# Two graph-attention layers on one core: bias vectors loaded as rows, late broadcasts, and a new order of the first and last pairs

## The chip, the cores and the metric

The kernel runs on one core of one Trainium2 chip. The metric is device time in microseconds (us), the median over runs; lower is better. The engines are TensorE (PE, with its weight loads shown apart as PEld), VectorE (DVE), ScalarE (ACT), GpSimd (POOL) and SyncE (SP, which here only issues DMA transfers). ACT and POOL can issue transfers too, each on a queue of its own.

## The reference

The input x holds 128 graphs of 128 nodes with 512 features, all in float32. Two layers follow each other.

```
q, k, v = x @ Wq + bq, x @ Wk + bk, x @ Wv + bv        # 8 heads of 64
attn    = softmax(q k^T / 8 + (adj - 1) * 1e9)
y       = layernorm(x + (attn v) @ Wo + bo)
h       = y @ W
e       = leaky_relu(h a1 (rows) + h a2 (columns)) * adj
out     = layernorm(y + elu(softmax(e) h + beta * h))
```

`adj` is one 128 x 128 matrix of zeros and ones for all graphs, `a` is split into a1 and a2, `beta` is one number.

## The kernel before

The graphs are worked on in pairs: 64 pairs (`NG`), g = 0 to 63, each of graphs b0 and b1. The five products with 512 x 512 weights (named q, k, v, w for Wo, h for W) are done in seven block products each instead of eight, after a scheme of sums and differences of blocks. `product(name, g, n)` issues the block product n (1 to 7) on PE; `block_sum` makes the sums of the activations on POOL; `weight_sum(name, n, engine)` makes the sums of the weights, once, at the start: those of q and k on DVE, those of v, w and h on POOL. `take_part` moves a block of the result out of PSUM (on ACT for q, k, v and h, with the bias for q and k; on DVE for w), and `add_block` adds a second block to it on DVE.

A pair passes through these steps: its blocks of x are loaded (`fetch_blocks`, into a single buffer `xblk`) and turned by DVE (`turn_x`); the products of q and k; `scores` on PE; `mask` and `row_max` on DVE; `exps` and `normalise` on ACT; a write to DRAM and a read back that moves blocks (`attn_write`, `attn_read`), turned by DVE (`turn_attn`); v's products; `attend` on PE and `attend_evict` on ACT with v's bias; w's products; `residual`, which adds bo to x on POOL; the first layer norm; the edge weights of the second layer (`row_product`, `edge`, `leaky`, `weights`); `aggregate`; h's products; the ELU and the second layer norm; the store. In the last pair some products are done plainly (`plain`, `end_product`), since a second copy of half a weight can be loaded over a weight that is done with (`load_again`).

The order of the work is written out by hand as a list of pieces, each with a place, which is a number. `at(place, fn, ...)` records a piece, and at the end all pieces are sorted by place and issued in that order. A place is only a key: nothing on the chip waits for it, but each engine works through its own pieces in that order. The pair g has its places at `g * STEP + place` with STEP = 36.678. `rows(g)` holds the places of an ordinary pair; `other` holds tables of places of its own for pairs 0, 1, 2, 3, 60 and 61, in the order of `rows(g)`; `last_rows(g)` holds the pieces and places of pairs 62 and 63. The weights and constants of the start are recorded one by one below them (lines 1098 to 1137).

The loads of the start, by queue:

- SP: half of the first pair's blocks (L81), Wq (L99), then, behind a `memset` on DVE that follows the first `turn_x` (`load_k_and_v`, L205), Wk and Wv; then x of the first pair, the second pair's blocks, W and Wo (L119).
- ACT: the other half of the first pair's blocks.
- POOL: two columns for the biases of q and k (`column`, L107: 512 numbers spread over 128 partitions, four on each), `adj`, and then `load_later` (L150), placed at the very start: the column for v's bias and the broadcasts of beta, a1, a2 and bo to all partitions (`broadcast`, L102).

The first user of the biases is `take_part` (L352) for q and k and `attend_evict` (L463) for v. `make_beta` (L167) uses beta, `wa_column` (L175, eight pieces on DVE), `wa_turn` (PE) and `wa_centre` (DVE) turn W and a into two rows; bo is used by `residual` (L429). `keep_busy` (L131) issues 15 matmuls of the identity with itself on PE at the start, whose result nobody reads.

Of the kernel before, what the change touches and what calls it, by code (L numbers as in the profile page):

```python
# [8 lines left out]
F32 = mybir.dt.float32  # L9
# [4 lines left out]
P = 128  # L14
# [8 lines left out]
def gnn_two_layers(  # L23
# [34 lines left out]
    nc = tc.nc  # L58
# [48 lines left out]
    def column(src, name):  # L107
        t = cpool.tile([P, NC], F32, tag=name, name=name)
        nc.gpsimd.dma_start(out=t, in_=src.rearrange("(c p) -> p c", p=P))
        return t  # L110

    wv_sb, wq_sb, wk_sb = turned("wv_sb"), turned("wq_sb"), turned("wk_sb")
    xblk, xn = {0: load_blocks(0)}, {}
    load_turned(wq_sb, wq)
# [16 lines left out]
    def keep_busy(n, name):  # L131

        t = ps_mm.tile([P, P], F32, tag="mm", name=name)
        for _ in range(n):
            nc.tensor.matmul(t, ident, ident, start=True, stop=True)

    keep_busy(15, "early")
    mhalf = cpool.tile([P, G], F32, tag="mhalf", name="mhalf")
    nc.gpsimd.memset(mhalf, -0.5)
    bq_c = column(bq, "bq_c")  # L140
    bk_c = column(bk, "bk_c")
# [8 lines left out]
    def load_later():  # L150
        later["bv"] = column(bv, "bv_c")
# [306 lines left out]
    def attend_evict(b):  # L458

        oT[b] = wk2.tile([P, NC, N], F32, tag="oT", name=f"oT_{b}")  # L460
        src = po.pop(b)
        for c in range(NC):
            nc.scalar.activation(  # L463
                oT[b][:, c, :], src[:, c, :], AF.Identity, bias=later["bv"][:, c : c + 1]
            )
# [352 lines left out]
    def last_rows(g):  # L818

        b0, b1 = g * G, g * G + 1  # L820
        if g == NG - 2:
# [4 lines left out]
                (-24.602, product, "q", g, 1), (-21.007, take_part, "q", g, 1, 0, 0),  # L826
                (-20.065, product, "q", g, 6), (-18.272, product, "q", g, 7),
                (-17.379, product, "k", g, 7), (-17.337, take_part, "q", g, 6, 1, 0),
                (-16.541, fetch_x, b0), (-16.486, product, "q", g, 2), (-16.091, fetch_x, b1),
                (-15.593, product, "k", g, 1), (-14.7, product, "k", g, 2),  # L830
                (-12.947, take_part, "k", g, 1, 0, 0), (-12.481, add_block, "q", g, 2, 0, 0),
                (-12.121, add_block, "k", g, 2, 0, 0), (-10.901, residual, b0),
                (-9.651, residual, b1), (-9.477, product, "q", g, 5),
                (-8.344, take_part, "q", g, 5, 1, 1), (-7.718, product, "k", g, 6),
                (-6.585, take_part, "k", g, 6, 1, 0), (-5.093, product, "k", g, 5),
                (-3.799, take_part, "k", g, 5, 1, 1), (-3.334, product, "q", g, 3),
                (-2.499, add_block, "k", g, 7, 1, 1), (-2.441, product, "k", g, 3),
                (-2.201, take_part, "q", g, 3, 0, 1), (-2.139, add_block, "q", g, 7, 1, 1),
                (-1.548, product, "k", g, 4), (-1.308, take_part, "k", g, 3, 0, 1),
                (-0.655, product, "q", g, 4), (0.478, add_block, "q", g, 4, 1, 0),  # L840
                (1.178, add_block, "k", g, 4, 1, 0), (2.175, scores, b1), (3.322, scores, b0),
                (3.562, mask, b1, 0), (4.182, mask, b1, 1), (4.222, product, "v", g, 1),
                (4.802, mask, b0, 0), (5.285, product, "v", g, 2), (5.422, mask, b0, 1),
                (6.042, row_max, b0), (6.391, take_part, "v", g, 1, 0, 0), (7.182, row_max, b1),
                (7.382, exps, b0, 0), (7.883, product, "v", g, 6), (8.152, exps, b0, 1),
                (8.922, exps, b0, 2), (9.122, add_block, "v", g, 2, 0, 0), (9.692, exps, b0, 3),
                (10.462, exps, b1, 0), (10.481, product, "v", g, 7), (10.682, row_inv, b0),
                (11.232, exps, b1, 1), (12.002, exps, b1, 2), (12.772, exps, b1, 3),
                (13.793, row_inv, b1), (15.553, normalise, b0, 0), (16.143, normalise, b0, 1),
# [322 lines left out]
```

## Time and profile before

| what | value |
|---|---|
| median of 3 runs | 2377.96 us (2376.72 to 2378.68) |
| the profiled execution | 2381.36 us |
| its span, from first to last instruction | 2379.6 us |
| PE busy | 2353.9 us (99%) |
| DVE busy | 1960.5 us (82%) |
| ACT busy | 1589.5 us (67%) |
| POOL busy | 867.7 us (36%) |
| moved by DMA | 269.83 MB, mean 113 GB/s |

The page of the profile gives the busy time of each engine, the chain of work that ended last, followed back from the last instruction, and the costliest groups of instructions. Beside it the trace answers questions: the timeline lists instructions in order of time with their start, their duration and, in brackets, how long the engine had been idle before and what released it; busy time can be asked for any stretch of the span; the view of the DMA queues gives packets, megabytes and the share of the 16 DMA engines' time, also for a stretch. The queues are q1 for SP, q10 for ACT and q0 for POOL. "x30" after a line is a count of instructions; a float32 matmul appears as two.

### The profile page before, as it was taken

Reading aid. Unit: us, or ns where it says so; the run is one execution under the profiler, and the core shown is the slowest. Engines: PE = TensorE matmul, PEld = TensorE weight load, DVE = VectorE, ACT = ScalarE, POOL = GpSimd, SP = SyncE. Lnnn points to the kernel's source line nnn. Section 1 sums busy time; section 2 is a strip of 40 time slices with the busy share of each in tenths; the row PEclk is TensorE's granted clock in tenths of the full one; section 3 lists DMA queues with packets and bytes.
Section 4 is the critical chain, followed back from the end, with each engine's and each line's share of the span. In section 5 each row is a group of like instructions: output and inputs, shape, how many; then the busy total and the mean of one; then the engine's idle time right before and its main releaser. Section 6 shows DMA issues by size and latency. Waiting matters only on the chain.

```text
span 2379.6 us, 50867 instructions
## 1 busy us (share of the span) xinstructions
PE 2353.9 (99%) x17702; PEld 2177.3 (91%) x17702; DVE 1960.5 (82%) x4390; ACT 1589.5 (67%) x5762; POOL 867.7 (36%) x1047
## 2 busy tenths in 40 slices
PE   8999999999999999999999999999999999999997
PEld 7999899999999999999999999999999999999986
DVE  6787788888888888888888888888888888888887
ACT  4675666766766667667666676676666766766765
POOL 6243333433433334334333333343343333433432
PEclk9999999999999999999999999999999999999999
DMA  6333334334333343343433433424434334333432
GB/s 192 107 92 119 111 107 125 95 118 128 97 119 116 105 122 103 109 134 92 120 119 103 122 108 109 127 91 121 123 102 118 110 109 125 96 117 124 114 115 73
DMA packets 256193, 269.83 MB, mean 113 GB/s; under 512 B 57456, under 2 KB 204912, under 8 KB 255552
## 3 DMA queue, kind: packets, MB, share of 16 engines
q1 hardware_dynamic: 254992, 265.45, 37.1%
q8 instruction: 140, 2.29, 0.4%
q0 software_dynamic: 400, 0.86, 0.1%
q14 instruction: 117, 0.96, 0.1%
q10 hardware_dynamic: 544, 0.26, 0.0%
HBM read 157.62 MB, written 108.85 MB: 112 GB/s over the span
## 4 chain that ended last, share of the span: by engine, by line
PE 95%; DMA 2%; DVE 1%; ACT 1%; issue 0%; SPq 0%; POOLq 0%; POOL 0%; ACTq 0%; DVEq 0%
PE pk L304 12%; PE pq L304 12%; PE pv L298 12%; PE ph L298 11%; PE pw L298 11%; PE eq L304 9%; PE psc L376 5%; PE po L451 5%; PE pz L639 5%; PE eh L298 4%; PE ew L298 4%; PE ev L298 4%; DMA w_sb<-in_L_gnn_W_dram 1%; DMA wk_sb<-in_L_gnn_Wk_dram 0%; DMA scr<-sb 0%
## 5 line engine op out<-in xcount | busy, mean ns | idle before, releaser
L432 POOL TENSOR_TENSOR x<-x,bo_b_in 128x512 f32<-128x512 f32 x128 | 163.3, 1277 | 858.6 <-DMA x<-in_x_dram 858.6
L398 ACT ACTIVATE s<-s,nmax 128x128 f32<-128x128 f32 x1024 | 396.9, 396 | 58.3 <-DVE nmax L392 58.2
L412 ACT ACTIVATE sb<-s,rinv 128x128 f32<-128x128 f32 x1024 | 325.2, 392 | 0.4 <-DVE rinv L405 0.4
L352 ACT ACTIVATE kT<-pk,bk_c 128x128 f32<-128x128 f32 x512 | 159.7, 363 | 204.3 <-PE pk L304 146.2
L352 ACT ACTIVATE qT<-pq,bq_c 128x128 f32<-128x128 f32 x512 | 160.1, 367 | 156.7 <-PE pq L304 156.7
L502 DVE SCALAR_TENSOR_TENSOR ya<-w,wa_row 128x512 f32<-128x512 f32 x256 | 223.9, 874 | 4.4
L398 ACT ACTIVATION_READ_ACCUMULATOR s<-s,nmax 128x1 f32 x1024 | 199.2, 195 | 0.0
L463 ACT ACTIVATE oT<-po,bv_c 128x128 f32<-128x128 f32 x512 | 139.1, 382 | 80.2 <-PE po L451 80.1
L349 DVE TENSOR_TENSOR w<-pw,x 128x256 f32<-128x256 f32 x252 | 106.4, 422 | 99.8 <-PE pw L298 94.0
L441 DVE STREAM_TRANSPOSE attnT<-ab 128x512 f32<-128x512 f32 x256 | 172.6, 693 | 7.5 <-DMA ab<-scr 7.2
L384 DVE SCALAR_TENSOR_TENSOR s<-psc,amask 128x512 f32<-128x512 f32 x256 | 168.7, 681 | 0.8 <-PE psc L376 0.8
L392 DVE TENSOR_REDUCE nmax<-s 128x8 f32<-128x1024 f32 x128 | 156.1, 1220 | 4.4
L346 ACT COPY h<-ph 128x256 f32<-128x256 f32 x252 | 93.7, 372 | 94.9 <-PE ph L298 94.7
L346 ACT COPY v<-pv 128x256 f32<-128x256 f32 x256 | 94.4, 369 | 86.4 <-PE pv L298 59.9
L237 DVE STREAM_TRANSPOSE xT<-xblk 128x512 f32<-128x512 f32 x128 | 139.7, 1110 | 6.2 <-DMA xblk<-in_x_dram 6.2
L257 POOL TENSOR_TENSOR tx<-xT 128x256 f32<-128x256 f32 x128 | 95.6, 748 | 124.3 <-PE psc L376 104.3
L654 DVE SCALAR_TENSOR_TENSOR u<-h,x 128x512 f32<-128x512 f32 x126 | 87.1, 691 | 63.7 <-ACT h L346 61.6
L304 PE MATMUL pq<-xT,wq_sb 128*128 128x128 f32 x1024 | 135.1, 275 | 3.0 <-DMA wq_sb<-in_L_gnn_Wq_dram 3.0
L304 PE MATMUL pk<-xT,wk_sb 128*128 128x128 f32 x1024 | 135.9, 277 | 2.1 <-DMA wk_sb<-in_L_gnn_Wk_dram 2.1
L298 PE MATMUL pv<-wv_sb,xT 128*128 128x256 f32 x512 | 137.5, 392 | 0.0
L304 PEld LDWEIGHTS pk<-xT,wk_sb 128*128 128x128 f32 x1024 | 130.2, 193 | 5.5 <-DMA wk_sb<-in_L_gnn_Wk_dram 2.3
L304 PEld LDWEIGHTS pq<-xT,wq_sb 128*128 128x128 f32 x1024 | 129.3, 192 | 6.4 <-issue 3.2
(677 smaller groups left out, 6349.8 us busy)
## 6 DMA issues: line engine op xcount, KB each, us to landing
scr<-sb SPq DMA_DIRECT2D x128, 512.0 KB
ab<-scr SPq DMA_DIRECT2D x512, 128.0 KB
x<-in_x_dram SPq DMA_DIRECT2D x128, 256.0 KB
xblk<-in_x_dram SPq DMA_DIRECT2D x254, 128.0 KB
out_dram<-u SPq DMA_DIRECT2D x126, 256.0 KB
pb<-s2d SPq DMA_DIRECT2D x62, 128.0 KB
attd<-att SPq DMA_DIRECT2D x62, 128.0 KB
ab<-attd SPq DMA_DIRECT2D x248, 32.0 KB
```

What stands on the lines that cost most here:

```text
L237: nc.vector.transpose(xT[g][:, :, t * N : (t + 1) * N].rearrange("p m (b r) -> p b m r", r=Q), xblk[g][:, t].rearrange("p b (c m) -> p b m ...
L298: nc.tensor.matmul(out, b[:, c, :], a[:, c, :], start=first and c == 0, stop=(c == 1), skip_group_check=True,)
L304: nc.tensor.matmul(out[:, m * N : (m + 1) * N], a[:, c, m * P : (m + 1) * P], b[:, c, :], start=first and m == 0 and c == 0, stop=(c == 1) ...
L346: nc.scalar.copy(dst, src)
L352: nc.scalar.activation(dst[:, m, :], src[:, m * N : (m + 1) * N], AF.Identity, bias=BIAS[name][:, 2 * i + m : 2 * i + m + 1],)
L384: nc.vector.scalar_tensor_tensor(s_t[b][:, j * HP : (j + 1) * HP, :], psc[b][j], SCALE, amask.rearrange("p (o n) -> p o n", o=1).broadcast ...
L392: nc.vector.tensor_reduce(nmax[b], s_t[b], AX.X, ALU.max, negate=True)
L398: nc.scalar.activation(s_t[b][:, h, :], s_t[b][:, h, :], AF.Exp, bias=nmax[b][:, h : h + 1], accum_out=rsum[b][:, h : h + 1],)
L412: nc.scalar.mul(sb[b][:, :, h, :], s_t[b][:, h, :].rearrange("p (b c) -> p b c", c=Q), rinv[b][:, h : h + 1],)
L432: nc.gpsimd.tensor_tensor(xr[b], xr[b], later["bo"], ALU.add)
L441: nc.vector.transpose(attnT[b].rearrange("p h (a r) -> p a h r", r=Q)[:, rows], ab[b].rearrange("p a (h c) -> p a h c", c=Q)[:, rows],)
L502: nc.vector.scalar_tensor_tensor(z, y[b], 1.0, wa_row[j], ALU.mult, ALU.mult, accum_out=s12[g][:, i, j : j + 1])
```

## The change

The three biases of q, k and v are no longer loaded as columns by POOL. They are loaded as 12 rows of 128 numbers by ACT's queue, behind its half of the first blocks; PE turns them behind the matmuls of `keep_busy`, in the same PSUM tile, and ACT copies the 128 x 12 result to SBUF. Slices of it serve as the three bias columns.

`load_later` now holds only the four broadcasts, and moves from the first place to a place behind the last of v's weight sums. With it move the pieces that use what it loads: `make_beta`, all eight `wa_column`, both `wa_turn` and `wa_centre`, and the `residual` pieces of the first two pairs. Wo is loaded before W, and the second pair's blocks are fetched before the second x.

The places of the first pairs (0 and 1 wholly, 2 and 3 in part) and of the last four (60 and 61 from some place on, 62 and 63 wholly) are other numbers. The pieces themselves are the same ones, apart from those named above. Pairs 4 to 59 keep their places.

```diff
-    def column(src, name):
-        t = cpool.tile([P, NC], F32, tag=name, name=name)
-        nc.gpsimd.dma_start(out=t, in_=src.rearrange("(c p) -> p c", p=P))
-        return t
-
     wv_sb, wq_sb, wk_sb = turned("wv_sb"), turned("wq_sb"), turned("wk_sb")
     xblk, xn = {0: load_blocks(0)}, {}
+
+    bias_rows = cpool.tile([3 * NC, P], F32, tag="bias_rows", name="bias_rows")
+    for i, src in enumerate((bq, bk, bv)):
+        nc.scalar.dma_start(
+            out=bias_rows[i * NC : (i + 1) * NC], in_=src.rearrange("(c p) -> c p", p=P)
+        )
     load_turned(wq_sb, wq)
...
-
-    keep_busy(15, "early")
+        return t
+
+    early = keep_busy(15, "early")
+    nc.tensor.transpose(early[:, : 3 * NC], bias_rows, ident[: 3 * NC, : 3 * NC])
+    bias_c = cpool.tile([P, 3 * NC], F32, tag="bias_c", name="bias_c")
+    nc.scalar.copy(bias_c, early[:, : 3 * NC])
     mhalf = cpool.tile([P, G], F32, tag="mhalf", name="mhalf")
     nc.gpsimd.memset(mhalf, -0.5)
-    bq_c = column(bq, "bq_c")
-    bk_c = column(bk, "bk_c")
+    bq_c, bk_c, bv_c = (bias_c[:, i * NC : (i + 1) * NC] for i in range(3))
...
     def load_later():
-        later["bv"] = column(bv, "bv_c")
         later["beta"] = broadcast(cpool, beta, 1, "beta_b")
...
-                oT[b][:, c, :], src[:, c, :], AF.Identity, bias=later["bv"][:, c : c + 1]
+                oT[b][:, c, :], src[:, c, :], AF.Identity, bias=bv_c[:, c : c + 1]
...
-            (20.046, turn_attn, b0, 0), (20.106, normalise, b1, 3), (20.666, turn_attn, b0, 1),
+            (20.404, normalise, b1, 2), (20.484, turn_attn, b0, 0), (20.994, normalise, b1, 3),
...
-            (62.027, end_store, b1, 1), (62.477, end_store, b1, 0),
+            (62.815, end_store, b1, 1), (63.265, end_store, b1, 0),
...
-    at(0.583, load_later)
-    at(5.685, load_k_and_v)
-    at(8.723, weight_sum, "q", 3, nc.vector)
...
-    at(12.183, make_beta)
-    at(13.163, weight_sum, "k", 3, nc.vector)
...
-    at(16.043, make_mask)
-    at(16.793, load_weight, w1_sb, w1)
-    at(19.323, weight_sum, "v", 3, nc.gpsimd)
-    at(19.493, load_weight, wo_sb, wo)
...
-    at(21.883, wa_column, 0, 0)
-    at(22.613, wa_column, 0, 1)
...
-    at(24.623, wa_column, 0, 3)
-    at(25.353, weight_sum, "v", 4, nc.gpsimd)
...
-    at(38.807, wa_centre, 1)
...
+    at(3.885, load_k_and_v)
+    at(6.923, weight_sum, "q", 3, nc.vector)
...
+    at(10.383, make_mask)
+    at(11.363, weight_sum, "k", 3, nc.vector)
...
+    at(14.243, weight_sum, "v", 3, nc.gpsimd)
+    at(14.293, load_weight, wo_sb, wo)
...
+    at(17.693, load_weight, w1_sb, w1)
+    at(18.863, weight_sum, "v", 4, nc.gpsimd)
+    at(20.143, load_later)
...
+    at(31.963, make_beta)
+    at(32.483, wa_column, 0, 2)
...
+    at(38.463, wa_centre, 0)
+    at(43.373, wa_column, 1, 0)
+    at(44.303, weight_sum, "h", 1, nc.gpsimd)
+    at(44.303, wa_turn, 1)
+    at(45.493, wa_centre, 1)
```

## The prediction

> **What bounds the kernel now.** I read the page first: PE is busy 99% of the span and carries 95% of the chain that ended last, so only stretches in which PE idles, or works on nothing useful, can give time back. Busy time by stretch shows where they are: from 200 to 2200 us PE is busy 1997.06 of 2000 us, and the losses sit in the first 60 us and in the last 60. The rows below are such stretches (us from the start, then PE, PEld, DVE, ACT and POOL busy, PE clock, DMA share, GB/s).
>
> ```profile
> 0.00:11.20 11.20, 5.51 (x31) 5.35 (x31) 2.25 (x4) 1.28 (x1) 8.80 (x21) 1.00 0.69 183
> 11.20:20.70 9.50, 7.40 (x48) 7.20 (x49) 6.17 (x11) 1.25 (x4) 0.00 (x0) 0.82 1.03 343
> ...
> 28.80:54.00 25.20, 23.89 (x188) 21.85 (x186) 23.74 (x45) 16.64 (x68) 17.20 (x16) 1.00 0.47 128
> 54.00:70.00 16.00, 16.00 (x134) 14.31 (x133) 12.16 (x24) 12.88 (x56) 5.57 (x8) 1.00 0.31 98
> 15.00:20.00 5.00, 3.70 (x20) 3.71 (x21) 2.90 (x5) 0.43 (x2) 0.00 (x0) 0.69 1.05 314
> ```
>
> Before 11.2 us PE does only warming matmuls. From 11.2 to 20.7 it lacks 2.1 us, and from 15 to 20 its clock was 0.69. From 28.8 to 54 DVE is busy 23.74 of 25.2 us: there DVE is nearly as tight as PE, which is the main doubt below. From 54 us PE is full.
>
> The timeline of the start names what PE waited for:
>
> ```profile
> 1.31 0.93 POOL L109 DMA_DIRECT2D bq_c<-in_L_gnn_bq_dram  x1 [0.34 <-issue]
> ...
> 2.69 5.51 PE L135 MATMUL early<-ident 128*128 128x128 f32 x30 [2.69 <-POOL ident masks.py:199]
> ...
> 11.20 1.13 PE L304 MATMUL pq<-xT,wq_sb 128*128 128x128 f32 x8 [3.00 <-DMA wq_sb<-in_L_gnn_Wq_dram]
> ...
> 16.30 3.23 PE L304 MATMUL pk<-xT,wk_sb 128*128 128x128 f32 x16 [2.10 <-DMA wk_sb<-in_L_gnn_Wk_dram]
> ...
> 19.32 1.55 PE L304 MATMUL pq<-tx,s_q 128*128 128x128 f32 x8
> ...
> 20.70 1.06 PE L304 MATMUL eq<-tx,s_k 128*128 128x128 f32 x8
> ```
>
> The first useful product runs at 11.20, when Wq has landed; the fourth, at 16.30, when Wk has. After these two waits the clock is low: the three products k1, k2, q6 (k1 being product 1 of k) take 16.30 to 20.70 = 4.40 us, where three take 3 x 0.893 = 2.68 later. Why Wq needs from 1.67 (issue) to 11.08 is in the DMA view by queue, from 6 to 8 us and from 8 to 10 us (packets, MB, share of the 16 engines):
>
> ```profile
> q1 hardware_dynamic: 49, 0.34, 44.6%
> q0 software_dynamic: 57, 0.02, 39.1%
> ```
>
> ```profile
> q0 software_dynamic: 91, 0.11, 35.4%
> q1 hardware_dynamic: 26, 0.16, 20.9%
> ```
>
> POOL's queue (q0) takes 39.1% and 35.4% of the engines while it moves 0.02 and 0.11 MB: what it carries first are the three bias columns, 2 KB each, that landed 7.7 to 8.2 us after issue. Wq meanwhile falls from 0.48 MB in 4 to 6 us to 0.34 and 0.16 MB.
>
> At the other end of the run the timeline shows DVE's turn of the attention waiting for its round trip through DRAM, and PE behind it:
>
> ```profile
> 2326.22 0.34 SPq L419 DMA_DIRECT2D scr<-sb  x1
> ...
> 2335.82 1.30 DVE L441 STREAM_TRANSPOSE attnT<-ab 128x512 f32<-128x512 f32 x2 [2.29 <-DMA ab<-scr]
> ...
> 2337.22 0.43 PE L533 MATMUL pb<-ident,s_in 128*128 128x128 f32 x2 [1.60 <-DVE s_in L510]
> ```
>
> **What the skill says.** "DMA: Bandwidth & Descriptors", Specifications, gives 512 B as the smallest transfer for line rate, with a read-modify-write below; the columns are pieces of 4 B, and the trace agrees (39.1% of the engines for 0.02 MB). The same page, Queues, rings and completion order: each DMA engine takes turns between its queues, packet by packet; so POOL's packets slow SP's, as q1's fall shows. Its section on the anatomy of a GpSimd-issued DMA prices one at 2.0 us + bytes / 436 GB/s, 2.6 us for 256 KB; here such broadcasts took 10.1 to 14.2 us beside SP's backlog, so that is only the lower bound. "TensorE: Matmul & The Clock Gate", Part 1: an idle window of about 3.4 us halves the clock, sustained work restores it; the 0.69 after waits of 3.0 and 2.1 us agrees.
>
> **The change part by part.**
>
> 1. Bias loads. Three column loads leave POOL (0.93 + 0.79 + 0.75 = 2.47 us of issue, no one waits there) and become three row loads on ACT's queue, 12 runs of 512 B. ACT issued two loads in 0.93 us, so three cost 1.4 us of an ACT that is idle until 9.06. Added: one small transpose on PE behind the warming matmuls (the nearest row, four of them for the weight vectors, took 0.68 us: 0.2) and one ACT copy (0.4, with its table load of 1.28 ahead of it). The copy runs at about 8.5 to 10, ahead of the first eviction of q, which is not yet due. Cost on the path: 0.2.
>
> 2. Wq. By 6 us SP's queue has moved half of it: 0.30 MB in 2 to 4 us, less 0.26 of the first blocks, and 0.48 in 4 to 6. The other 0.53 MB takes 1.3 us at 410 GB/s (0.61 MB at 74.9% in 12 to 14 us) or 2.2 at the 243 of 4 to 6 us: landing at 7.5 to 8.8 with about half a microsecond to complete; I take 8.2. PE's warming ends at 8.20 anyway, so the first product starts at 8.5: **-2.7** (-2.4 to -2.9).
>
> 3. Wk. The broadcasts (0.77 MB), issued at the start in the kernel before, are gone from this stretch too. 1.05 MB at 410 GB/s is 2.6 us, at 270 3.9: landing at 10.8 to 12.1 after Wq. PE reaches it after three products, 8.5 + 2.7 = 11.2, so the wait of 2.10 becomes 0 to 0.9: **-2.1 + 0.2**.
>
> 4. Clock. With no idle of that length left the 4.40 - 2.68 = **-1.7** come back (0 if a wait of 2 us stays).
>
> 5. The new order of the first pairs. Up to place 60 both orders hold the same 57 PE pieces, 50.8 us of work; in the trace they take from 11.20 to 68.66, so 6.6 us are lost: 2.1 and 1.7 as above, 0.35 + 0.42 + 0.88 waiting for evictions and sums, 1.2 in small gaps. I keep the last four. New is DVE's load: `make_beta`, eight `wa_column` (0.69 to 1.41 each, 0.77 mostly) and two `wa_centre` (2.0) now come between places 31.9 and 47.5, where three columns were done by 24.6. DVE's work between places 30 and 50, by durations from the timeline: 7 block additions of 0.42, 2 masks of 0.65, 4 half turns of the attention of 0.65, 2 turns of x of 1.1, 8 columns of 0.77, 2 centrings of 2.0, two reciprocals and `make_beta` of 0.7 in all, 19.9 us in 20 us of places; before, with 9 additions, 3 masks and 5 columns, 18.9. Against that, DVE is idle about 11 us between 5 and 28 and gets Wq and Wk earlier, and the columns run beside less POOL work. Cost 0 to 3, I take **+1.3**: what is late is the sum of k4 of the second pair, and with it the scores of the third.
>
> 6. `load_later` behind v's sums. Four broadcast issues (0.55 + 1.08 + 0.54 = 2.2 us) come on POOL after Wv (2.6 us after Wk, about 13.8), four sums of 1.3 and a block sum of 0.75, at 19.8 to 22. Behind them on POOL are Wo's sums, not needed before 50. First to need them is `make_beta`, behind the first reciprocal on DVE (39.32 before, about 33.5 then); with latencies of 8.4 to 11.5 they land at 28 to 33. Cost 0, covered by 0 to 5 us. The residuals that wait for bo move to place 37.6 and later; before, POOL stood 11.06 us at one of them with v's sums behind it.
>
> 7. SP's queue. The second pair's blocks now go ahead of the second x, Wo ahead of W. All land earlier, since 0.77 MB of broadcasts and the columns are behind or gone: Wo from 32.9 to about 20 (Wv at 13.8, then 1.8 MB of x, blocks and Wo at the 290 GB/s of 20.7 to 28.8 us). Cost 0.
>
> 8. Middle: the same rows, PE full; 0.
>
> 9. Last pairs. Same PE work. The keys of the order end 0.8 later (63.265 against 62.477), which bounds the loss by order alone. But the transfers decide the middle of this stretch: the write of the first attention is placed at 12.752 against 12.773, so the turn still comes near 2335.8 less the head's gain; from `spread_s2` on both orders have 36.3 us of PE work and gaps by their places. **+0.1**, from -1.0 to +1.2.
>
> Sum: -2.7 - 2.1 + 0.2 - 1.7 + 0.2 + 1.3 + 0.1 = -4.7. The profiled execution took 2381.36 us (span 2379.6, 1.8 around it), 3.4 above the median shown; it would be 2376.7, and the median 2377.96 - 4.7 = **2373.3**. A run differs from another of this kernel by up to 0.1%, so about 0.2% (4.8 us) is what can be told from no change: the forecast stands on that line.
>
> **Rivals.**
>
> A, full gain: DVE keeps up. For it speaks its early idle. -6.0: 2371.9.
>
> B, DVE becomes the bound between 30 and 50 us: its 23.74 of 25.2 us speak for it. Then the part of the head's gain that exceeds DVE's own earlier start is lost, about 3 to 4 us: 2376.2.
>
> C, the columns were not what held Wq: the first blocks' 512 B runs and the 243 GB/s speak for it, q0's 39.1% against. Half of 2, 3 and 4 is left, -3.2 + 1.6 = -1.6: 2376.4.
>
> D, slower: the broadcasts, issued late, hold DVE at `make_beta`, and with it the sums that PE's scores need. Each microsecond past 33.5 costs one; from 38 on the gain is gone. At 41, 19 us after issue, 2381. Against it: the longest landing seen is 14.2, and SP's backlog ends near 26.
>
> **How the numbers follow.** Forecast (2372.3 to 2375) 0.40, A 0.20, B 0.20, C 0.12, D 0.05, a last stretch that loses several us 0.03. Faster by over 0.2% (below 2373.2): all of A, half of the forecast and a little of B: 0.42. Slower: D and the last stretch, partly: 0.06. Same: 0.52. The range, 2370.8 to 2377.4, leaves out the slower cases and the edge of A. The forecast alone: 2372.3 to 2375.
>
> **What would show it.** First useful matmul near 8.5, Wk's wait under 1 us, clock near 1.0 from 15 to 20, q0 almost empty before 19 us; the 57 pieces ending near 63.8 instead of 68.66; PE's wait for kT and qT near 45 us as the place of step 5. It is wrong if Wq lands after 9.5, if DVE waits for beta or a, or if PE's idle after 2320 grows by over 1.5 us.

## The result, and the profile after

The changed kernel took 2382.61 us (median of 22 runs, 2380.45 to 2385.48), the kernel before, measured beside it, 2379.89 (22 runs, 2376.72 to 2384.1). The ratio is 1.0013, with a 95% interval of 1.0007 to 1.0019: slower by 0.13%, where 2373.3 with a range of 2370.8 to 2377.4 was forecast. The sign was wrong. The profiled execution of the changed kernel took 2381.45 us with a span of 2379.7, that of before 2381.36 with 2379.6, so the two traces compared here differ by 0.1 us while the medians differ by 2.7: a trace is one execution, and single executions lie up to 2 to 4 us on either side of their median.

Busy time by stretch of the changed kernel, for the rows shown of before (us from the start, then PE, PEld, DVE, ACT and POOL busy, PE clock, DMA share, GB/s):

```profile
0.00:11.20 11.20, 7.27 (x48) 7.05 (x49) 4.07 (x6) 1.45 (x2) 3.71 (x13) 1.00 0.80 254
11.20:20.70 9.50, 8.70 (x77) 8.50 (x76) 8.77 (x13) 3.75 (x12) 6.32 (x5) 1.00 1.06 315
...
28.80:54.00 25.20, 23.25 (x192) 20.86 (x188) 24.10 (x45) 17.27 (x70) 15.76 (x14) 1.00 0.40 129
54.00:70.00 16.00, 15.61 (x117) 14.09 (x118) 12.20 (x29) 14.26 (x60) 5.00 (x7) 1.00 0.22 70
15.00:20.00 5.00, 4.20 (x37) 4.00 (x36) 4.38 (x6) 2.15 (x8) 4.84 (x5) 1.00 1.11 274
```

PE is busy 8.70 of 9.5 us where it had 7.40, with a clock of 1.00 from 15 to 20 us (0.69 before). From 28.8 to 54 and from 54 to 70 it now has less than before (23.25 against 23.89, 15.61 against 16.00), beside a DVE of 24.10 of 25.2.

The timeline of the start of the changed kernel:

```profile
1.70 0.60 ACTq L112 DMA_DIRECT2D bias_rows<-in_L_gnn_bq_dram  x1
...
2.53 5.19 PE L136 MATMUL early<-ident 128*128 128x128 f32 x30 [2.53 <-POOL ident masks.py:199]
...
8.10 0.20 PE L140 MATMUL early<-ident,bias_rows 12*128 12x12 f32 x1 [0.37 <-DMA bias_rows<-in_L_gnn_bv_dram]
...
9.32 2.02 PE L307 MATMUL pq<-xT,wq_sb 128*128 128x128 f32 x16 [1.02 <-DMA wq_sb<-in_L_gnn_Wq_dram]
...
12.07 1.95 PE L307 MATMUL pk<-xT,wk_sb 128*128 128x128 f32 x16
...
17.59 1.16 PE L307 MATMUL pk<-tx,s_k 128*128 128x128 f32 x8 [0.80 <-DVE kT L365]
```

Bias rows go out on ACT's queue; the first useful product starts at 9.32 (11.20 before), k's first at 12.07 without a wait (16.30 before, after a wait of 2.10). New is a wait of 0.80 for a sum on DVE, which is explained below, with the runs on DVE. The DMA queues from 6 to 8 us, and then from 8 to 10:

```profile
q1 hardware_dynamic: 92, 0.70, 98.4%
...
q0 software_dynamic: 8, 0.00, 0.2%
```

```profile
q1 hardware_dynamic: 100, 0.75, 90.0%
```

SP's queue moves 0.70 and 0.75 MB in these stretches (0.34 and 0.16 before) and POOL's has all but gone. At the other end, the timeline of the lines shown of before:

```profile
2325.47 0.34 SPq L422 DMA_DIRECT2D scr<-sb  x1
...
2333.82 1.30 DVE L444 STREAM_TRANSPOSE attnT<-ab 128x512 f32<-128x512 f32 x2 [0.65 <-DMA ab<-scr]
...
2335.46 0.38 PE L536 MATMUL pb<-ident,s_in 128*128 128x128 f32 x2
```

The write of the attention goes out at 2325.47, the turn comes at 2333.82, and PE has no wait at `pb` any more (1.60 before). So this place, which the prediction took for the one that decides the tail, got better.

What got worse lies 60 to 80 us earlier. A steady marker is the start of a pair's `scores` on PE (pairs counted from 0; "the fourth pair" in the expectations below is pair 3). From these starts in the timelines:

| kernel | pair 3 | pair 61 | 61 to 62 | 62 to 63 | 63 to end of span |
|---|---|---|---|---|---|
| before | 120.06 | 2241.09 | 38.07 | 34.99 | 65.4 |
| changed | 116.89 | 2237.52 | 40.59 | 37.19 | 64.4 |

The head brought pair 3 ahead by 3.2 us, and pair 61 still by 3.6. Between the scores of pairs 61 and 62 the changed kernel loses 2.5 of that. The next stretch takes 2.2 more, but PE has no wait in it in either kernel: it is mostly order, since both `attend` of pair 62 (1.9 us of PE's work) now stand ahead of pair 63's scores. At the end 1.0 comes back.

That it is no more has to do with this one execution. From 2361 to 2365 us the clock was 0.57, and two of PE's products took 2.00 and 1.89 us, where they take 1.13 and 1.03 in the tail alone (below). Of six executions with the new last pairs (the changed kernel, tail alone, early broadcasts, no columns, and two that are edited between 2240 and 2280), this one and that of no columns have such a drop; in the four without it the last column is 62.7. None of the seven with the last pairs of before (one of them packed) has one until the last 6 us. These are too few to say that the new order brings it.

PE's waits in the first of these stretches, from the timeline, of before:

```profile
2271.56 1.16 PE L304 MATMUL pk<-tx,wk_sb 128*128 128x128 f32 x8 [0.72 <-ACT kT L352]
```

and of the changed kernel:

```profile
2257.34 1.10 PE L301 MATMUL ph<-s_h,th 128*128 128x256 f32 x4 [1.01 <-DVE h L365]
...
2272.30 1.16 PE L307 MATMUL pq<-xT,s_q 128*128 128x128 f32 x8 [1.17 <-ACT qT L355]
2274.23 1.16 PE L307 MATMUL eq<-tx,wq_sb 128*128 128x128 f32 x8 [0.77 <-DVE qT L365]
```

Before, PE waits 0.72 us in all, now 1.01 + 1.17 + 0.77 = 2.95, each time for an eviction (the move of a product out of PSUM, or the sum with it) by ACT or DVE of a product that lies in the same PSUM tile as the next one. What DVE did ahead of the last of them, in the changed kernel:

```profile
2268.59 0.42 DVE L365 TENSOR_TENSOR kT<-eq,kT 128x256 f32<-128x256 f32 x1 [1.81 <-PE eq L307]
...
2269.38 1.12 DVE L240 STREAM_TRANSPOSE xT<-xblk 128x512 f32<-128x512 f32 x1
2270.42 1.25 DVE L657 SCALAR_TENSOR_TENSOR u<-h,x 128x512 f32<-128x512 f32 x2
2271.59 1.09 DVE L240 STREAM_TRANSPOSE xT<-xblk 128x512 f32<-128x512 f32 x1
2272.60 1.26 DVE L444 STREAM_TRANSPOSE attnT<-ab 128x512 f32<-128x512 f32 x2
2273.79 0.39 DVE L365 TENSOR_TENSOR qT<-eq,qT 128x256 f32<-128x256 f32 x1
```

DVE stood 1.81 us for a product of PE, then worked without a break through two turns of x, the ELU and a turn of the attention, and only behind these came the sum of q (2273.79) for which PE stood until 2274.23. Busy time from 2240 to 2280 us says the same: PE 39.13 us before and 36.95 after, DVE 34.95 and 27.62. Neither engine was short of time; each waited for the other's queue.

### The profile page after: what moved, and what is told of

It reads as the page before. It is cut to its first block, busy times and chain, and to the rows that moved or that the text cites. A ratio compares the mean times of both kernels' runs of the same rounds, so it can differ in the third digit from the quotient of the medians.

```text
span 2379.7 us, 50860 instructions
## 1 busy us (share of the span) xinstructions
PE 2355.7 (99%) x17703; PEld 2176.2 (91%) x17703; DVE 1960.0 (82%) x4390; ACT 1591.8 (67%) x5763; POOL 866.5 (36%) x1044
## 3 DMA queue, kind: packets, MB, share of 16 engines
q1 hardware_dynamic: 254992, 265.45, 37.6%
## 4 chain that ended last, share of the span: by engine, by line
PE 96%; DVE 2%; DMA 1%; ACT 1%; issue 0%; SPq 0%; POOL 0%; POOLq 0%; DVEq 0%; ACTq 0%
PE pv L301 12%; PE pk L307 12%; PE pq L307 12%; PE ph L301 11%; PE pw L301 11%; PE eq L307 9%; PE psc L379 5%; PE po L454 5%; PE pz L642 5%; PE eh L301 4%; PE ev L301 4%; PE ew L301 4%; DMA ab<-scr 0%; DMA wq_sb<-in_L_gnn_Wq_dram 0%; PE plh L671 0%
## 5 line engine op out<-in xcount | busy, mean ns | idle before, releaser
L355 ACT ACTIVATE kT<-pk,bias_c 128x128 f32<-128x128 f32 x512 | 160.2, 364 | 195.8 <-PE pk L307 144.7
L355 ACT ACTIVATE qT<-pq,bias_c 128x128 f32<-128x128 f32 x512 | 160.6, 368 | 157.1 <-PE pq L307 157.1
L466 ACT ACTIVATE oT<-po,bias_c 128x128 f32<-128x128 f32 x512 | 139.5, 382 | 85.3 <-PE po L454 85.3
L260 POOL TENSOR_TENSOR tx<-xT 128x256 f32<-128x256 f32 x128 | 95.3, 745 | 134.6 <-PE psc L379 103.3
L379 PE MATMUL psc<-kT,qT 64*128 64x128 f32 x2048 | 132.6, 279 | 0.1
```

Of the source, the lines that this page charges most:

```text
L355: nc.scalar.activation(dst[:, m, :], src[:, m * N : (m + 1) * N], AF.Identity, bias=BIAS[name][:, 2 * i + m : 2 * i + m + 1],)
L379: nc.tensor.matmul(psc[b][j][:, m, :], qT[g][feats, m, rows], kT[g][feats, m, rows], start=True, stop=True,)
```

## The experiments

Theory T: the new places of the last four pairs give back what the head gains, in the stretch from 2240 to 2280 us. Rival H: the head's gain is lost elsewhere, or isn't there. Each kernel was timed beside the kernel before, whose median was 2379.07, 2379.20, 2379.02 and 2379.49 us in the four batches. Each start of scores quoted is from one execution.

**The head alone, the tail alone.** The first kernel is the changed one with the tables of pairs 60 and 61 and `last_rows` of before, the second the reverse.

```diff
 # e1_head_only, against the changed kernel; e2_tail_only: the same edit of the kernel before, with the new numbers
-        other[NG - 4], other[NG - 3], last_rows(g): the new places
+        other[NG - 4], other[NG - 3], last_rows(g): the places of before
```

> The changed kernel with the earlier places for the last four pairs (60 to 63). Theory T, the last pairs' new places give back what the head gains: scores of pair 61 start about 3.6 us earlier than in the kernel before, as in the changed kernel, and the end too, so 3 to 4 us faster than before (ratio about 0.9986). Rival H, the head's lead is lost in the middle or is there only in one profiled execution: no better than the changed kernel, ratio 1.000 to 1.0015.

> The kernel before with only the new places of the last four pairs. Theory T: 3.5 to 6 us slower than before (ratio 1.0015 to 1.0025), with PE's waits for qT, h and eq between 2250 and 2285. Rival H: within 1 us of before. A second rival, that the new places of the last pairs suffer only because they are reached 3.6 us earlier against the same transfers: within 1.5 us of before as well, while the head alone gains.

Head alone: 2378.24 us (13 runs), ratio 0.9994 (0.9986 to 1.0002); pair 61 at 2237.16, the next scores 37.89 later. Tail alone: 2382.40 us (21 runs), ratio 1.0015 (1.0008 to 1.0021); pair 61 at 2239.93, the next scores 40.59 later, exactly as in the changed kernel, though it gets there 2.4 us later than that one. Its timeline:

```profile
2259.75 1.10 PE L298 MATMUL ph<-s_h,th 128*128 128x256 f32 x4 [1.01 <-DVE h L362]
...
2274.72 1.16 PE L304 MATMUL pq<-xT,s_q 128*128 128x128 f32 x8 [1.17 <-ACT qT L352]
2276.64 1.16 PE L304 MATMUL eq<-tx,wq_sb 128*128 128x128 f32 x8 [0.77 <-DVE qT L362]
```

T holds for the tail, and the second rival of e2 (that the tail suffers only when reached early) falls: the same three waits with the same lengths appear with the old head. The tail costs 3.3 us by the medians, a little under the 3.5 to 6 expected. The head's part of T holds at most in its sign: 0.8 us by the medians instead of 3 to 4, and the interval reaches from a gain of 3.3 us to a loss of 0.5.

**Pairs 62 and 63 alone put back.**

```diff
 # against the changed kernel; the tables of pairs 60 and 61 stay new
-        last_rows(g): the new places
+        last_rows(g): the places of before
```

> The changed kernel with the earlier places for the last two pairs (62 and 63) alone; pairs 60 and 61 keep the new ones. Theory T1, the loss comes where DVE holds PE, between 2250 and 2285, from the places of pairs 60 and 61: still 2 us or more slower than the kernel with all four pairs put back, so about the time of before (ratio 0.9995 to 1.001). Rival T2, the loss is in the last two pairs' own places: as fast as with all four put back, ratio about 0.9986.

2394.23 us, ratio 1.0059 (1.0046 to 1.0072): neither theory had this. The distances are 42.87 and 40.97 us, with PE's longest waits in the timeline at

```profile
2276.10 1.16 PE L307 MATMUL pk<-xT,s_k 128*128 128x128 f32 x8 [2.18 <-ACT kT L355]
...
2305.09 1.31 PE L307 MATMUL pq<-tx,wq_sb 128*128 128x128 f32 x8 [3.14 <-ACT qT L355]
```

The places of pairs 60 and 61 and those of 62 and 63 interleave on every engine; that half of one order clashes with half of the other is an explanation that fits and was not tested. The run can't assign the loss to one pair's table; it has to be sought in the order that results.

**Spread the products, and pack them.** Pair 62's products were moved so that others lie between a product and the next one in the same region; in the second kernel the order of before was packed in the same way.

```diff
 # e6_products_spread, against the changed kernel, pair 62
-(-19.172, product, "q", g, 2)            (-5.066, product, "q", g, 5)
+(-17.5, product, "q", g, 2)              (-8.7, product, "q", g, 5)
-(-3.933, take_part, "q", g, 5, 1, 1)     (-3.015, add_block, "q", g, 7, 1, 1)
+(-7.2, take_part, "q", g, 5, 1, 1)       (-5.2, add_block, "q", g, 7, 1, 1)
 # e7_products_packed, against the kernel before, pair 62
-(-18.272, product, "q", g, 7)   (-17.379, product, "k", g, 7)   (-16.486, product, "q", g, 2)
+(-18.4, product, "q", g, 7)     (-18.38, product, "k", g, 7)    (-18.36, product, "q", g, 2)
-(-9.477, product, "q", g, 5)    (-8.344, take_part, "q", g, 5, 1, 1)
+(-3.4, product, "q", g, 5)      (-3.36, take_part, "q", g, 5, 1, 1)
```

> The changed kernel with two products of pair 62 moved in PE's order (q's second behind h's second, q's fifth ahead of k's seventh, with its eviction and the sum behind it), so that other products lie between a product and the next one that overwrites its PSUM region. Theory T, too little lies between: the waits of 1.01, 1.17 and 0.77 us between 2255 and 2280 shrink to less than 1 us together, scores of pair 62 follow those of pair 61 by 38 to 38.5 us instead of 40.6, and the time falls by 2 to 2.5 us, to about 2380.3. Rival, DVE or the attention's round trip holds this stretch anyway: the waits come back under other names, the distance stays above 40 us and the time within 0.7 us of 2382.6.

> The kernel before with the opposite edit in pair 62: q's seventh and second and k's seventh product ahead of h's first, q's fifth directly ahead of q's third. Theory T: waits of about 1.0 and 1.2 us appear there, the distance of the scores of pairs 61 and 62 grows from 37.9 to about 40 us and the time by 1.5 to 2.5 us (ratio 1.0006 to 1.0010). Rival: PE's slack elsewhere takes them up, distance within 0.5 us of 37.9, ratio within 0.0003 of 1.

Packed: 2381.31 us, ratio 1.0010 (1.0001 to 1.0018), distance 40.12 us. The same wait for `h` as in the changed kernel appears in the timeline, to the hundredth, and one for q:

```profile
2261.00 1.10 PE L298 MATMUL ph<-s_h,th 128*128 128x256 f32 x4 [1.01 <-DVE h L362]
...
2273.83 1.16 PE L304 MATMUL pq<-xT,s_q 128*128 128x128 f32 x8 [0.72 <-ACT qT L352]
```

So packing alone, with all else as before, costs 2.1 us in either measure (the interval of the time reaches from 0.2 to 4.3). Spreading the products alone failed: distance 40.31, median 2381.19, ratio 1.0010 (1.0002 to 1.0019), which against the kernel before is only 0.7 us less than the changed kernel loses. The wait for `h` was gone, but others took its place:

```profile
2257.30 1.16 PE L307 MATMUL pq<-xT,wq_sb 128*128 128x128 f32 x8 [0.99 <-ACT qT L355]
...
2274.82 1.16 PE L307 MATMUL eq<-tx,wq_sb 128*128 128x128 f32 x8 [1.92 <-DVE qT L365]
```

The 1.92 is again the sum of q on DVE: its last operand was evicted by 2270.0, but it still stood behind the same two turns of x and the ELU and ran at 2274.38. The 0.99 is q's second product, now waiting for the eviction of the first. Moving PE's pieces isn't enough where the eviction stands in a queue that is bunched.

**The whole stretch.** To the spread products were added q's first eviction, v's third product of pair 61 and the turns of x of pair 63, all put where the order of before has them.

```diff
 # against the kernel with the products spread
-(-17.887, take_part, "q", g, 1, 0, 0)     # pair 62
+(-21.0, take_part, "q", g, 1, 0, 0)
-            28.987, ...  30.093, ...      # pair 61: product v 3 and its eviction
+            25.469, ...  26.575, ...
-(-43.353, turn_x, g, 0), (-42.323, turn_x, g, 1)   # pair 63
+(-46.849, turn_x, g, 0), (-45.459, turn_x, g, 1)
```

> The changed kernel with, between the scores of pairs 61 and 62, q's first eviction, q's second and fifth product with their evictions and sums, v's third product of pair 61, and the turns of x of pair 63 put where the kernel before has them in that order. Theory T (the stretch loses by PE waiting for evictions that DVE and ACT do late, because their own queues are bunched there): the waits shrink from 2.9 to about 1 us, the distance of the scores falls from 40.6 to 38 to 39 us, and the time by 1.5 to 2.5 us, to 2380 to 2381. Rival, another wait takes their place as it did when the products alone were spread: distance above 40 us, time within 1 us of 2382.6.

2379.45 us, ratio 1.0000 (0.9992 to 1.0008), distance 38.45. One wait is left in the stretch:

```profile
2272.73 1.16 PE L307 MATMUL eq<-tx,wq_sb 128*128 128x128 f32 x8 [1.32 <-DVE qT L365]
```

Against 1.0013 for the changed kernel this is 3.1 us back, of which 2.1 are the distance; the rest is not located. T is confirmed from both sides, in its later form: products packed too tightly, and evictions that stand in bunched queues. Which of the pieces moved here was needed beside the spread products was not taken apart.

**The head in parts.** First the biases as rows alone, with the broadcasts at the start and all places as before; then the changed kernel with the broadcasts put back to place 0.583; then the kernel before with six matmuls more, in the wait for Wk.

```diff
 # e3_rows_only, against the kernel before: column() and its three loads replaced
+    bias_rows = ...; nc.scalar.dma_start(...) x3; transpose behind keep_busy; nc.scalar.copy(bias_c, ...)
 # e5_early_broadcasts, against the changed kernel
-    at(20.143, load_later)
+    at(0.583, load_later)
 # e8_warm, against the kernel before (k's first product has place 12.183)
+    at(12.181, keep_busy, 6, "warm")
```

> The kernel before with only the biases of q, k and v loaded as rows and turned; the broadcasts stay at the start and every place stays. If the columns were what held the weights of q back: they land near 9 to 9.5 and the first useful matmul starts about 1.5 to 2 us earlier than 11.20; the place of PE's first 57 pieces moves by 1.5 to 2.5 us, and the time falls by 1.5 to 2.5 us (ratio 0.9990 to 0.9994). If the late broadcasts were: first matmul within 0.5 us of 11.20 and ratio within 0.0005 of 1.

> The changed kernel with the broadcasts issued at their place of before (0.583), all else as changed. If late broadcasts are what lets the weights of q and k land early: q's weights land near 10 to 11 instead of 9.2 and k's wait is back with 1 to 2 us; the scores of the fourth pair, at 116.5 to 117.4 us in the kernels with the new head, come up to 2 us later, or at the same time if DVE holds them anyway as the kernel with rows alone suggests (117.0 there). Time: 0 to 2 us above the changed kernel, 2382.6 to 2384.6.

> The kernel before with six more matmuls of the identity ahead of k's first product, to be run while PE waits for k's weights; nobody reads their result. If the cold clock after that wait cost about 1.7 us and is the larger part of what the rows alone gained: clock 1.0 from 15 to 20 us, scores of the fourth pair near 117.5 to 118 instead of 119.2 to 120.1, time 1 to 1.7 us below before (ratio 0.9993 to 0.9996). If the clock is seldom cold, or what is won is lost behind DVE: ratio within 0.0003 of 1.

Rows alone: 2378.31 us, ratio 0.9995 (0.9987 to 1.0003). Early broadcasts: 2385.34 us, ratio 1.0024 (1.0014 to 1.0034), 2.7 us above the changed kernel where at most 2 were expected, with pair 3 at 121.14. Warm: 2378.47 us, ratio 0.9998 (0.9989 to 1.0006), pair 3 at 118.98. The timelines, of the rows alone:

```profile
9.51 0.20 PE L139 MATMUL early<-ident,bias_rows 12*128 12x12 f32 x1 [1.84 <-DMA bias_rows<-in_L_gnn_bv_dram]
10.86 1.13 PE L306 MATMUL pq<-xT,wq_sb 128*128 128x128 f32 x8 [1.15 <-DMA wq_sb<-in_L_gnn_Wq_dram]
...
15.28 2.05 PE L306 MATMUL pk<-xT,wk_sb 128*128 128x128 f32 x16 [1.35 <-DMA wk_sb<-in_L_gnn_Wk_dram]
```

of the early broadcasts:

```profile
10.61 2.02 PE L307 MATMUL pq<-xT,wq_sb 128*128 128x128 f32 x16 [1.24 <-DMA wq_sb<-in_L_gnn_Wq_dram]
...
15.79 2.05 PE L307 MATMUL pk<-xT,wk_sb 128*128 128x128 f32 x16 [2.26 <-DMA wk_sb<-in_L_gnn_Wk_dram]
```

and of the tail alone, which has the whole head of before, columns too:

```profile
9.51 1.13 PE L304 MATMUL pq<-xT,wq_sb 128*128 128x128 f32 x8 [0.88 <-DMA wq_sb<-in_L_gnn_Wq_dram]
...
15.12 3.78 PE L304 MATMUL pk<-xT,wk_sb 128*128 128x128 f32 x16 [2.46 <-DMA wk_sb<-in_L_gnn_Wk_dram]
```

With the columns, the first product started at 9.51, 10.26, 10.79 and 11.20 us in four executions (tail alone, packed, warm, before); without them but with early broadcasts at 10.86 and 10.61; without both between 9.02 and 10.15 in eight, six of them below 9.4. So the columns are not seen to hold Wq, though only two executions without them have the broadcasts early. The broadcasts hold Wk: k's first product starts between 15.12 and 16.30 us with them early (where no matmuls were put ahead of it), between 11.80 and 13.32 with them late. What the rows gained in the trace (pair 3 at 117.01, against 120.06, 119.22 and 117.54 in the three executions with the old head) stands beside a clock of 1.00 from 15 to 20 us, against 0.69, 0.50 and 0.66; but 117.54 was reached with 0.66, so the clock is not shown to be its cause. The run that was to price this clock doesn't: its clock fell earlier, while PE waited for Wq, and q's first three products took 1.64, 1.91 and 1.41 us instead of 1.1.

**DVE between 30 and 50 us.** First the column products left out (the rows for the edge weights are then not computed); then, with the tail of before, PE's turn of the first attention row moved back; then, also with the tail of before, POOL's residuals moved away from the columns.

```diff
 # e10_no_columns, against the changed kernel
-    at(..., wa_column, j, c)   # all eight
+    at(20.1, lambda: nc.gpsimd.memset(wa_col, 0.0))
 # e11_turn_later, against the head alone
-    at(35.603, wa_turn, 0)
+    at(37.95, wa_turn, 0)
 # e12_residuals_later, against the head alone; residuals of graphs 0, 1, 2, 3 at 44.35, 44.4, 66.0 and 66.5
-    37.593, 38.843 (pair 0)    3.415, 5.445 (pair 1)
+    44.35, 44.4 (pair 0)       29.322, 29.822 (pair 1)
-    at(45.583, weight_sum, "h", 2, nc.gpsimd)    at(46.863, weight_sum, "h", 4, nc.gpsimd)
+    at(54.5, weight_sum, "h", 2, nc.gpsimd)      at(54.6, weight_sum, "h", 4, nc.gpsimd)
```

> The changed kernel without the eight column products of DVE for the two attention rows (the columns are set to zero by GpSimd instead, so the edge weights are not those of the reference); the turn and the centring of the rows stay. It takes 8.9 us of DVE's work out of the stretch from 33 to 48 us. If DVE's load there is what eats the head's lead: the waits for the turn (0.9) and for the attention's turn (1.0) go, the scores of the fourth pair start at 114 to 115.5 us instead of 116.5 to 117.4, and the time falls by 1.5 to 2.5 us below the changed kernel, to 2380 to 2381. If PE's own work or another engine holds that stretch: within 0.7 us of 116.9, and of 2382.6.

> The changed kernel with the earlier places for the last four pairs, and with PE's turn of the first attention row moved from place 35.603 to 37.95, behind v's third product, so that PE does not wait there for DVE's column products (1.06 us with the last pairs put back and no other edit, 0.9 in the changed kernel). If that wait counts: scores of the fourth pair near 115.7 us and the time about 0.8 us below that kernel's 2378.2, ratio to before 0.9988 to 0.9993. If the attention's turn on DVE takes it back: 116.5 and a ratio of 0.9994 or so.

> The kernel with the new head and the earlier places for the last four pairs (2378.2 us), with the four residual additions of pairs 0 and 1 on POOL behind the first of h's weight sums (two of them) and behind w's block sums (the other two), and h's last two weight sums behind those too: POOL is then idle while DVE does its column products. In that kernel the first four columns took 1.77, 1.64, 1.09 and 1.63 us beside the residuals, the later ones 0.69. If it is POOL's work beside them that stretches them: all eight take about 0.7, DVE is 3.4 us ahead at 41 us, PE's waits for the turn (1.06) and for the attention's turn (about 1.0) shrink, and the scores of the fourth pair start at 114.5 to 115.5 instead of 116.5, the time falls by 1 to 2 us to 2376.2 to 2377.2 (ratio 0.9988 to 0.9992). If the columns are slow by themselves, or PE is held by something else: durations and 116.5 as they were, ratio 0.9994 to 0.9997.

No columns: 2381.29 us, 1.3 below the changed kernel (ratio 1.0007, 1.0001 to 1.0014); between the first theory's 1.5 to 2.5 and the second's 0.7. Set against the kernel before in their own batches, the two are 2.3 and 2.7 above it, so the times alone don't decide. The scores of pair 3 start at 116.16, only 0.7 earlier, but in this execution those of pair 0 had started 1.1 later (26.08 against 24.99), and from there to pair 1's at 51.68 it took 25.6 us where the changed kernel took 26.7. It took 25.6 as well in the last kernel here, which has all eight columns. So the columns as they stand in the changed kernel cost PE about 1 us there. The turn moved back: 2377.69 us, ratio 0.9997 (0.9989 to 1.0005), pair 3 at 116.81. The wait for the turn went, but the waits for sums of k grew from 0.80 us in the head alone to 1.3 in two waits, the longer 0.9 (us in all, times, longest), in the view of waits:

```profile
PE pk L307 <- DVE kT L365: 1.3, 2, 0.9
```

The rival was right: what DVE does late is waited for in one place or another. Why it is late is in the head alone's timeline, DVE's columns and the residuals on POOL beside them:

```profile
31.74 4.19 POOL L435 TENSOR_TENSOR x<-x,bo_b_in 128x512 f32<-128x512 f32 x3
...
33.02 1.77 DVE L180 SCALAR_TENSOR_TENSOR wa_t<-w_sb,uf_in 128x512 f32<-128x512 f32 x1
...
34.84 1.64 DVE L180 SCALAR_TENSOR_TENSOR wa_t<-w_sb,uf_in 128x512 f32<-128x512 f32 x1
...
35.89 1.17 POOL L260 TENSOR_TENSOR tx<-xT,tx 128x256 f32<-128x256 f32 x1
...
36.52 1.09 DVE L180 SCALAR_TENSOR_TENSOR wa_t<-w_sb,uf_in 128x512 f32<-128x512 f32 x1
...
37.02 1.71 POOL L435 TENSOR_TENSOR x<-x,bo_b_in 128x512 f32<-128x512 f32 x1
...
37.65 1.63 DVE L180 SCALAR_TENSOR_TENSOR wa_t<-w_sb,uf_in 128x512 f32<-128x512 f32 x1
...
39.33 0.69 DVE L180 SCALAR_TENSOR_TENSOR wa_t<-w_sb,uf_in 128x512 f32<-128x512 f32 x1
```

and in the kernel with the residuals moved:

```profile
31.95 0.72 POOL L260 TENSOR_TENSOR tx<-xT,tx 128x256 f32<-128x256 f32 x1
...
32.68 0.68 DVE L180 SCALAR_TENSOR_TENSOR wa_t<-w_sb,uf_in 128x512 f32<-128x512 f32 x1
...
33.40 0.69 DVE L180 SCALAR_TENSOR_TENSOR wa_t<-w_sb,uf_in 128x512 f32<-128x512 f32 x1
...
47.52 1.28 POOL L435 TENSOR_TENSOR x<-x,bo_b_in 128x512 f32<-128x512 f32 x1
```

Four columns took 6.13 us beside POOL's residuals and one of its block sums (L260), and 4 x 0.69 = 2.76 without them. The scores of pair 3 came 0.8 us sooner (115.70), and the time fell to 2376.91 us (21 runs), ratio 0.9989 (0.9982 to 0.9995): 2.6 us faster than the kernel before and 5.7 than the changed one. Against the head alone it is 1.3 by the medians, and 1.8 when each is set against the kernel before in its own batch. This is the best version: the new head, the residuals out of DVE's way, the old tail.

"SBUF — State Buffer", in the Trainium skill, section "Who interferes with whom", says that a DVE instruction with two inputs in SBUF contends with a GpSimd instruction that reads SBUF, and that the one which comes second blocks altogether. The columns have two such inputs (W and a), and the lines agree, down to the block. POOL's third residual ends at 31.74 + 4.19 = 35.93, and the column that started at 34.84 ends at 36.48; POOL's block sum ends at 37.06, and the column beside it at 37.61; POOL's next residual ends at 38.73, and its column at 39.28. Each column ends 0.55 us after the POOL instruction that ran when it started, whether it had begun 0.5 or 1.1 us before that end: it was not slowed but stood until POOL was nearly or wholly done. It works the other way too: the residual at 37.02, begun while a column ran, took 1.71 us instead of 1.28. Every column of over 0.7 us, in each of the traces that have columns, ends 0.55 us after such a POOL instruction (POOL's spans are rough in a profile, but a difference that is always the same is not chance).

So the trace of before already held the rule: its column of 1.41 us (37.25 to 38.66) ends 0.55 after POOL's `s_h` sum (36.80 to 38.11). And the 0.80 us for which PE stood at 17.59 in the changed kernel has the same origin. DVE's sums of k at 14.42 and 16.10 took 1.64 and 1.10 us instead of 0.69, ending 0.54 and 0.55 after POOL's sum of v (14.22, 1.30 us) and block sum (15.48, 1.17 us), and the sum that PE waited for came behind them. Before, POOL stood waiting at a residual in that stretch. To move these sums was not tried. With the residuals moved, one of the two sums of k happened to run free and that wait was 0.2, so part of the 0.8 us at pair 3 may be chance.

## Why the prediction was wrong

Two terms of its sum missed: the last pairs by 3.2 us (3.3 for 0.1), and the head, steps 1 to 6, by 4.0 (-0.8 by the medians for -4.8). Either miss alone would have left the sum negative (-1.5 or -0.7), a change slightly faster; together they turned the sign. The mechanism of the first is shown by the runs, that of the second only in part.

- **Step 9, the last pairs (+0.1, from -1.0 to +1.2): the step that failed by its mechanism.** It measured +3.3 us (tail alone). The working held that PE's work is the same and that the attention's round trip through DRAM decides. The round trip did get better (1.60 to 0 at `pb`). But the working compared only the ends of the order and the stretch from 2312 on; PE's clearance between a product, its eviction and the next product in the same PSUM tile was never counted along the new order from 2240 to 2280. Its own condition, PE's idle growing by over 1.5 us, was written for after 2320, and the loss is before it. Rival D, the slower one, had the wrong mechanism: nothing was held at `make_beta`.
- **Step 2, Wq (-2.7).** Measured -1.9 in the two traces (11.20 to 9.32), and 11.20 was the latest of four executions with the columns (the others 9.51 to 10.79); by the means of these four and of the eight with neither columns nor early broadcasts it is 10.4 to 9.4, -1.0. The cause was misjudged: as far as these executions show, rival C was right that the columns didn't hold Wq. (By the step's own terms Wq would land at 7.8 to 8.7, not 7.5 to 8.8; nothing hangs on it.)
- **Step 3, Wk (-2.1 + 0.2).** Right in the changed kernel (no wait); it is the late broadcasts that bring this, as e5 shows by undoing them. The turn-taking of the queues, which the prediction took from "DMA: Bandwidth & Descriptors", "Queues, rings and completion order", fits that. The price of 2.6 us for such a broadcast, from the same page, is a lower bound only, as the prediction said: in the changed kernel the two of a took 7.7 us from issue to landing, in the view of the queues.
- **Step 4, clock (-1.7).** It is 1.00 now. What it is worth was not isolated, since the run for it missed. Nor is the drop tied to the length of a wait as the prediction took it to be: after waits of 1.24 and 2.26 us the clock from 15 to 20 us was 1.00 (early broadcasts), after 1.22 and 1.87 it was 0.66 (packed). The 0.69 that the step started from is one execution.
- **Step 1 (+0.2).** The transposition took 0.20 and the copy 0.17 us; new was a wait for the rows, 0.37 in the changed kernel and 1.84 with rows alone, hidden behind Wq's landing or nearly so.
- **Step 5, DVE (+1.3, 0 to 3).** Right in kind, and rival B near: the 57 pieces ended at 65.5 where 63.8 was forecast; 0.8 of that is step 2, the rest, 0.9, makes this step about 2.2. The durations were the error: the columns were priced at 0.69 to 1.41, "0.77 mostly", and four of them took 1.09 to 1.77. They did not "run beside less POOL work": the residuals had been put beside them.
- **Step 6, the broadcasts (0).** The broadcasts themselves landed in time. But step 6 also noted the residuals' new place at 37.6 and gave them no price, and they are what held up three of the columns: 1.3 us by the medians of e12 and the head alone.
- **Step 7, SP's order (0).** Right: no wait for W or Wo is left on PE or DVE in the first 60 us.
- **Step 8, the middle (0).** Pair 3 to pair 61 took 2121.0 us before and 2120.6 after. One place in it isn't neutral, though. Around 250 us DVE waits for the attention's read, and what a lead brings can be lost there. DVE's lines in the head alone and in the version with the residuals moved:

```profile
253.05 0.71 DVE L444 STREAM_TRANSPOSE attnT<-ab 128x512 f32<-128x512 f32 x1 [3.02 <-DMA ab<-scr]
```

```profile
253.90 0.71 DVE L444 STREAM_TRANSPOSE attnT<-ab 128x512 f32<-128x512 f32 x1 [4.39 <-DMA ab<-scr]
```

The second came to pair 3 earlier by 0.8 us and to pair 61 later by 0.8 (2238.01 against 2237.16). These are single executions: that of the head alone was its fastest of 13 (2376.22), that of the other lay above its median (2377.56). From pair 5 to pair 8 the scores fall behind the steady 36.50 us a pair by 3.5 to 4.2 us in ten executions with either head, and by 4.6 to 5.3 in four with the new one.
- **The head's worth.** The prediction's -4.8 for steps 1 to 6 stands against -2.1 in the traces (pair 61 at 2238.0 as a mean of five executions with the new head, 2240.1 of three with the old) and -0.8 in the medians of the head alone. The interval of that, from -3.3 to +0.5, holds the -2.1 and not the -4.8. About 1.1 us of the shortfall is the trace that all of it was read from: pair 3 started at 120.06 there, the latest of the three with the old head, whose mean is 118.9. Why the times show less than the traces stays open; the wait around 250 us is one candidate, which was not tried.
- **The base.** The median of 3 runs that the forecast started from, 2377.96, was 1.9 us below that of 22. That moves the forecast to 2375.2, not across zero.

## What to carry to other kernels

When an order is searched anew, walk each engine's new queue and, for every buffer that is overwritten, count what lies between the writer, the eviction and the next writer; equal work and an equal last key say nothing about that. A piece moved for PE's sake helps only if the engine that evicts for it isn't bunched at that point. And price a moved piece by what runs beside it at its new place: here four additions on an engine that nobody waited for cost about 1.3 us, because of what they held up. The trace of before can tell this: an instruction that is now long and now short, and when long always ends by the same time after one of another engine, is waiting for it, though the profile counts it as busy.

## What the runs showed that was not expected

- POOL's additions beside DVE's column products: 1.77, 1.64, 1.09 and 1.63 us instead of 0.69, and POOL's residuals up to 1.73 instead of 1.28 us, each standing until the other's instruction had ended. Removing the overlap (h's last weight sums moved with it) was worth 1.3 us, more than the head's whole gain (0.8) by the medians.
- Half of a searched order put back (e4) cost 12 to 16 us more than either whole order behind the same head: 2394.23 against 2382.61 and 2378.24.
- Three 4-byte-piece column loads, at 39.1% of the DMA engines' time, were not seen to delay a megabyte on another queue (two executions without them), while 0.77 MB of broadcasts issued early delayed k's first product by about 2 to 4 us (15.12 to 16.30 against 11.80 to 13.32).
